# Products with adj by pairs of batches in seven half products, with one pool of PSUM banks

## The chip, the cores and the metric

The kernel runs on one core of a Trainium2 chip. The metric is the device time of one execution in microseconds (us), median of the runs in the fast state.

PE is TensorE, PEld its weight loads, DVE VectorE, ACT ScalarE, POOL GpSimd, SP the engine that issues the DMAs here (all but two loads of adj). PSUM is the memory that the kernel's matmuls write; its buffers there make eight banks of 512 fp32 columns. A record is one matmul entry of the trace; most fp32 matmuls leave two (1280 for the 640 product matmuls of the kernel before). L423 is line 423 of the kernel that the profile belongs to.

## The reference

Four graph layers on x (32 batches of 512 nodes and 128 features), each `x = x + layer(relu(layernorm(x)))`. The change concerns layer 1, a gated recurrence of five steps. Both of its matrices are `adj`, so a step needs one product with adj for each batch:

```python
def step(h, _):
    m_in = jnp.einsum('nm,bmd->bnd', in_matrix, h)      # in_matrix = out_matrix = adj
    m_out = jnp.einsum('nm,bmd->bnd', out_matrix, h)
    av = jnp.concatenate([m_in, m_out], axis=-1)
    u3 = h @ u3_w.T + u3_b
    z = jax.nn.sigmoid(av @ w3_w.T + w3_b + u3)
    r = jax.nn.sigmoid(av @ w4_w.T + w4_b + u3)
    hv = jnp.tanh(av @ w5_w.T + w5_b + (r * h @ u5_w.T + u5_b))
    h = (1.0 - z) * h + z * hv
    return (h, None)
h, _ = jax.lax.scan(step, input, None, length=time_step)   # five steps
```

Layer 0 is one normalized product with adj, layers 2 and 3 are graph attention. All is fp32.

## The kernel before

The kernel records every operation with an engine, an assumed cost, a due time and the values that it reads and writes. `Plan.run` then orders them once, when the program is built, as a list schedule. It hands out buffers as it goes, and the operations are emitted in that order. The tile framework adds the semaphore waits afterwards, from what the emitted instructions read and write.

```python
    plan = Plan({
        "bank": tiles(3, TOKENS, "bank", psum),
        "cand": tiles(1, TOKENS, "cand", psum),
        "wide": tiles(2, [P, C, 2 * P], "wide", psum),     # two banks each
        "lane": list(range(LANES)),                        # LANES = 4 batches in the recurrence at once
        ...
    def product(h, mT, due):
        p, m = Val("bank"), Val("m")
        for c in range(C):                                 # C = 4 chunks of 128 nodes
            op("PE", MM, due, lambda c=c: nc.tensor.matmul(flat(p.t), chunk(h, c), mT.t[:, c, :],
               start=(c == 0), stop=(c == C - 1)), ...)
        op("ACT", A, due, lambda: nc.scalar.copy(flat(m.t), flat(p.t)), r=[p], w=[m])
        return m
    ...
    def step(b, s, h, hT, due, lane):
        m = product(h, adjT, due)
        # PE: gate = w4*m + u3*hT   ACT: r = tanh(gate)   DVE: rh = (r + 1) * hT
        # PE: gate += w3*m (the same bank)   ACT: z = tanh(gate)
        # PE: cand = w5*m + u5*rh   ACT: hv = tanh(cand)   DVE: three operations make the new hT
        # DVE transpose, DMA out and in: h of the next step, floats of a chunk at stride four
```

The softmax here doesn't subtract the row's maximum and nothing guards it: scores larger than these inputs give would overflow.

## Time and profile before

The time was 1751.78 us (1751.01 to 1752.13, 4 runs).

| | before |
|---|---|
| PE busy | 99% of the span |
| DVE / ACT busy | 68% / 41% |
| start to start, fp32 record of 512 columns | 429 ns |
| start to start, record of 128 to 131 columns | 109 to 112 ns |
| weight load of h / of y | 308 / 190 ns (medians) |

The prediction below shows the lines. For PE, a duration in a group is a modelled latency, so its time is better read from the distance between starts. From each distance I subtracted what the columns take. That is an estimate, a line laid through the measured distances: 0.8333 x N + 2.3 ns for the N columns of a record. It gives 429 ns for 512 columns (measured 429), 111.5, 109.8 and 109.0 for 131, 129 and 128 (medians 112, shortest 111, 109 and 109), and in the changed kernel 215.6 for 256 (median 216). What remains is called excess below; I take it for the time in which PE had no columns to stream. It splits the span of 1749.9 us into 1687.8 of columns, 4.9 before the first matmul and 57.2 of excess: 15.5 in the first 100 us, 19.7 between 100 and 1600 us, 22.0 after.

### The profile page before, as it was taken

What the parts mean: (1) busy time and instruction counts of PE and PEld (TensorE: products, weight loads), DVE (VectorE), ACT (ScalarE), POOL (GpSimd) and SP (SyncE); (2) the same over time, 40 slices, a digit from 0 to 9 for tenths busy, and PEclk for the clock granted to TensorE, in tenths of its full rate; (3) what the DMA queues carried; (4) which work ended last, traced back from release to release, by engine and by line L of the source; (5) the groups of instructions that cost most, each with busy time, mean ns of one, the idle gap of its engine ahead of it and who ended that gap; (6) DMA issues with size and microseconds to landing.
All of it is one profiled execution on the core that took longest, in us unless ns stands there. A gap on an engine that the chain in (4) does not pass through costs nothing.

```text
span 1749.9 us, 20047 instructions
## 1 busy us (share of the span) xinstructions
PE 1724.1 (99%) x6256; PEld 1097.3 (63%) x6256; DVE 1182.3 (68%) x2853; ACT 711.4 (41%) x1389; POOL 184.5 (11%) x168
## 2 busy tenths in 40 slices
PE   7999999999999999999999999999999999999997
PEld 4555565756656666565666656666666666666576
DVE  8655566857767766585777756676767666666577
ACT  5433435334344343534344343344343443433342
POOL 5200001100101011110011110001100000000001
PEclk9999999999999999999999999999999999999999
DMA  6122223225233432323343233243233333333200
GB/s 187 37 66 66 67 72 100 76 69 141 69 102 87 107 103 67 98 75 78 100 109 103 73 81 89 61 114 99 71 86 88 91 95 83 83 91 87 59 6 25
DMA packets 199754, 146.96 MB, mean 84 GB/s; under 512 B 21600, under 2 KB 165088, under 8 KB 199648
## 3 DMA queue, kind: packets, MB, share of 16 engines
q1 hardware_dynamic: 199360, 145.16, 30.8%
q8 instruction: 49, 0.80, 0.2%
q10 hardware_dynamic: 288, 0.52, 0.1%
q14 instruction: 57, 0.47, 0.1%
HBM read 81.01 MB, written 64.60 MB: 83 GB/s over the span
## 4 chain that ended last, share of the span: by engine, by line
PE 96%; DVE 2%; ACT 1%; issue 0%; POOL 0%; DMA 0%; DVEq 0%; POOLq 0%; ACTq 0%
PE bank L423 38%; PE wide L559 13%; PE bank L467 8%; PE cand L474 8%; PE cand L475 8%; PE bank L460 8%; PE bank L461 8%; PE wide L524 3%; PE bank L439 2%; PE bank L403 1%; ACT y L387 0%; DVE e L552 0%; PE bank L544 0%; DMA e<-in_adj_dram 0%; PE bank L267 0%
## 5 line engine op out<-in xcount | busy, mean ns | idle before, releaser
L423 PE MATMUL bank<-adjT,h 128*128 128x512 f32 x1280 | 610.3, 603 | 3.2 <-ACT h L387 2.7
L423 PEld LDWEIGHTS bank<-adjT,h 128*128 128x128 f32 x1280 | 386.4, 310 | 166.8 <-issue 51.9
L479 DVE TENSOR_TENSOR hv<-hv,hT 128x512 f32<-128x512 f32 x160 | 111.2, 695 | 274.7 <-ACT hv L477 274.3
L377 POOL TENSOR_TENSOR rstd<-ve,mhalf 128x4 f32<-128x4 f32 x128 | 141.2, 1104 | 1341.8 <-DVE ve L375 1196.7
L559 PEld LDWEIGHTS wide<-h_gat,e 128*128 128x128 f32 x2048 | 241.2, 193 | 26.9 <-issue 20.6
L559 PE MATMUL wide<-h_gat,e 128*128 128x129 f32 x2048 | 242.3, 276 | 2.0 <-DVE v L565 2.0
L463 ACT ACTIVATE r<-bank,gate_bw 128x512 f32<-128x512 f32 x160 | 109.6, 685 | 257.0 <-PE bank L461 234.9
L425 ACT COPY m<-bank 128x512 f32<-128x512 f32 x192 | 112.1, 584 | 217.5 <-PE bank L423 217.1
L465 DVE SCALAR_TENSOR_TENSOR rh<-r,hT 128x512 f32<-128x512 f32 x160 | 110.3, 689 | 112.2 <-ACT r L463 111.5
L552 DVE SCALAR_TENSOR_TENSOR e<-row,h_gat,maskT 128x512 f32<-128x512 f32 x256 | 180.3, 744 | 2.9 <-DMA row<-line 2.5
L387 ACT ACTIVATE y<-x,off,rstd 128x128 f32<-128x128 f32 x384 | 163.2, 485 | 41.4 <-DVE off L384 21.8
L477 ACT ACTIVATE hv<-cand,gate_bw 128x512 f32<-128x512 f32 x160 | 109.7, 686 | 170.6 <-PE cand L475 170.6
L469 ACT ACTIVATE z<-bank,gate_bw 128x512 f32<-128x512 f32 x160 | 109.8, 686 | 149.5 <-PE bank L467 148.7
L467 PE MATMUL bank<-m,wT 128*128 128x512 f32 x320 | 163.9, 594 | 0.8 <-ACT r L463 0.8
L460 PE MATMUL bank<-m,wT 128*128 128x512 f32 x320 | 163.5, 593 | 0.7 <-ACT m L425 0.7
L474 PE MATMUL cand<-m,wT 128*128 128x512 f32 x320 | 163.4, 592 | 0.0
L461 PE MATMUL bank<-hT,wT 128*128 128x512 f32 x320 | 163.4, 592 | 0.0
L475 PE MATMUL cand<-rh,wT 128*128 128x512 f32 x320 | 163.4, 592 | 0.0
L411 DVE STREAM_TRANSPOSE sq<-hT 128x512 f32<-128x512 f32 x154 | 158.6, 1030 | 2.1
L423 PE MATMUL bank<-anT,y 128*128 128x512 f32 x256 | 121.8, 604 | 1.3 <-ACT y L387 1.3
L370 DVE BATCH_NORM_STATS2 st<-x 128x6 f32<-128x128 f32 x512 | 115.6, 278 | 2.2 <-DMA x<-in_x_dram 0.9
L482 DVE SCALAR_TENSOR_TENSOR hT<-hv,hT 128x512 f32<-128x512 f32 x160 | 112.0, 700 | 3.5
(90 smaller groups left out, 1307.8 us busy)
## 6 DMA issues: line engine op xcount, KB each, us to landing
far<-sq SPq DMA_DIRECT2D x840, 64.0 KB
h<-far SPq DMA_DIRECT2D x154, 256.0 KB
gT<-far SPq DMA_DIRECT2D x56, 256.0 KB
row<-line SPq DMA_DIRECT2D x56, 256.0 KB
x<-in_x_dram SPq DMA_DIRECT2D x32, 256.0 KB
out_dram<-x SPq DMA_DIRECT2D x32, 256.0 KB
far_mask<-mask SPq DMA_DIRECT2D x8, 128.0 KB
maskT<-far_mask SPq DMA_DIRECT2D x8, 128.0 KB
```

What stands on the lines that cost most here:

```text
L370: op("DVE", 0.21, due, lambda c=c: nc.vector.bn_stats(st.t[:, c, :], xb.t[:, c, :]), r=[xb[c]], w=[st[c]])
L377: op("POOL", 1.0, due, lambda: nc.gpsimd.tensor_tensor(rstd.t, ve.t, mhalf.t, ALU.pow), r=[ve, mhalf], w=[rstd])
L387: op("ACT", 0.32, due, lambda c=c: nc.scalar.activation(chunk(y, c), xb.t[:, c, :], AF.Relu, bias=off.t[:, c:c + 1], scale=rstd.t[:, c:c + ...
L411: op("DVE", 0.61 if form == "p q (c j) -> p q c j" else 1.0, soon, lambda: nc.vector.transpose(sq.t.rearrange(form, c=C), flat(src.t).rear ...
L423: op("PE", MM, due, lambda c=c: nc.tensor.matmul(flat(p.t), chunk(h, c), mT.t[:, c, :], start=(c == 0), stop=(c == C - 1)), r=[h[c] if len ...
L460: nc.tensor.matmul(flat(gate.t), gates.t[:, 0, :], flat(m.t), start=True, stop=False)
L461: nc.tensor.matmul(flat(gate.t), gates.t[:, 1, :], flat(hT.t), start=False, stop=True)
L467: op("PE", MM, due + 0.3, lambda: nc.tensor.matmul(flat(gate.t), gates.t[:, 2, :], flat(m.t), start=False, stop=True, skip_group_check=Tru ...
L474: nc.tensor.matmul(flat(cand.t), gates.t[:, 3, :], flat(m.t), start=True, stop=False)
L475: nc.tensor.matmul(flat(cand.t), u5T.t[:, 0, :], flat(rh.t), start=False, stop=True)
L552: op("DVE", 0.68, due + 3, lambda j=j: nc.vector.scalar_tensor_tensor(e.t[:, j, :], row.t, h.t[:, j, D + 1:D + 2], maskT[l].t[:, j, :], op ...
L559: nc.tensor.matmul(p.t[:, c, :D + 1], e.t[:, j, c * P:(c + 1) * P], h.t[:, j, :D + 1], start=(j == 0), stop=(j == C - 1))
```

## The change

Its intent is fewer columns on the full engine. Two batches of a step form a 2 x 2 block problem with adj, which one level of Strassen solves with seven half-size products in place of eight. The half products need four vector sums before and five after them. Six lanes (three pairs) replace four. Since a product now holds three banks, all eight banks become one pool: four tiles of two banks each, from which single banks and pairs are cut. h is laid out in pairs of floats. The shuttle of the diff is the transpose and the DMAs that turn the new hT into the next step's h.

```diff
-LANES = 4
+LANES = 6
@@ Plan.run
+        banks = [True] * (2 * len(self.buffers["psum"]))
+        def pick(v):
+            if v.kind == "wide":
+                return next(([i, i + 1] for i in range(0, len(banks), 2) if banks[i] and banks[i + 1]), None)
+            if v.kind == "bank":
+                some = [i for i, ok in enumerate(banks) if ok]
+                return [max(some, key=lambda i: (not banks[i ^ 1], i))] if some else None
+            return free[v.kind][-1:] or None
+        def take(v, slot):
+            ...
+                pair = self.buffers["psum"][slot[0] // 2]
+                v.t = pair if v.kind == "wide" else pair.rearrange("p (a c) (b k) -> p a (c b) k", a=2, b=2)[:, slot[0] % 2]
@@ buffers
-        "bank": tiles(3, TOKENS, "bank", psum),
-        "cand": tiles(1, TOKENS, "cand", psum),
-        "wide": tiles(2, [P, C, 2 * P], "wide", psum),
+        "psum": tiles(4, [P, C, 2 * P], "psum", psum),
@@ layout of h
-        return h.t.rearrange("p k (j c) -> p c (k j)", c=C)[:, c, :]
+        return h.t.rearrange("p a (f l) -> p a l f", l=2)[:, c // 2, c % 2, :]
@@ the bias add of layer 0 moves from POOL to DVE; the shuttle of h goes in two halves
@@ products of two batches
+        combine(S[2], x1[0], x2[0], sub)      # DVE, 128x256 each
+        combine(S[0], x2[0], x2[1], add)
+        combine(S[1], S[0], x1[0], sub)
+        combine(S[3], x1[1], S[1], sub)
+        times(r1, x1[0], 0, True, m1, m2, p1, u2, u4)      # PE, two matmuls of 256 columns each
+        op("ACT", ... copy(p1.t, low(r1)))
+        times(r2, S[1], 1, True)
+        op("DVE", ... tensor_add(u2.t, p1.t, low(r2)))
+        times(r3, S[0], 2, True)
+        op("DVE", ... tensor_add(u4.t, u2.t, low(r3)))
+        times(r1, x1[1], 3, False)
+        op("ACT", ... copy(low(m1), low(r1)))
+        times(r2, S[2], 4, True)
+        op("DVE", ... tensor_add(high(m2), u4.t, low(r2)))
+        times(r3, S[3], 5, False)
+        op("DVE", ... tensor_add(high(m1), u2.t, low(r3)))
+        times(r2, x2[1], 6, False)
+        op("DVE", ... tensor_add(low(m2), u2.t, low(r2)))
@@ (cut: seven factors of adj at the start, buffer counts, pairs in the main loop)
```

More of the change, by code (lines that the diff above doesn't have):

```diff
@@ L81, in run, with drop @@
     def run(self):
-        free = {k: list(reversed(v)) for k, v in self.buffers.items()}
+        free = {k: list(reversed(range(len(v)))) for k, v in self.buffers.items() if k != "psum"}
+        banks = [True] * (2 * len(self.buffers["psum"]))
[7 more added lines that the diff above has]
+        def take(v, slot):
+            v.slot = slot
+            if v.kind in ("wide", "bank"):
+                for i in slot:
+                    banks[i] = False
+                pair = self.buffers["psum"][slot[0] // 2]
+                v.t = pair if v.kind == "wide" else pair.rearrange("p (a c) (b k) -> p a (c b) k", a=2, b=2)[:, slot[0] % 2]
+            else:
+                free[v.kind].pop()
+                v.t = self.buffers[v.kind][slot[0]]
+        def drop(v):
+            if v.kind in ("wide", "bank"):
+                for i in v.slot:
+                    banks[i] = True
+            else:
+                free[v.kind].append(v.slot[0])
         ready = {e: [] for e in self.DELAY}
@@ L107, in start @@
                 opens = [v for v in o.vals if v.kind and v.t is None]
-                if all(free[v.kind] for v in opens):
-                    for v in opens:
-                        v.t = free[v.kind].pop()
+                got = []
+                for v in opens:
+                    if not (slot := pick(v)):
+                        break
+                    take(v, slot)
+                    got.append(v)
+                if len(got) < len(opens):
+                    for v in reversed(got):
+                        drop(v)
+                        v.t = None
+                else:
                     busy[e] = True
@@ L140, in run @@
                     if not v.uses and v.kind:
-                        free[v.kind].append(v.t)
+                        drop(v)
             for e in ready:
@@ L169, in gnn_stack @@
     plan = Plan({
-        "bank": tiles(3, TOKENS, "bank", psum),
-        "cand": tiles(1, TOKENS, "cand", psum),
-        "wide": tiles(2, [P, C, 2 * P], "wide", psum),
+        "psum": tiles(4, [P, C, 2 * P], "psum", psum),
         "lane": list(range(LANES)),
-        "x": tiles(16, TOKENS, "x"),
-        "h": tiles(LANES + 2, [P, Q, W * C], "h"),
+        "x": tiles(13, TOKENS, "x"),
+        "h": tiles(LANES + 1, [P, 2, 2 * D], "h"),
         "sq": tiles(2, [P, Q, W * C], "sq"),
         "far": tiles(4, [Q, W, Q, W * C], "far", dram),
-        "hT": tiles(2 * LANES, TOKENS, "hT"),
+        "hT": tiles(LANES + 3, TOKENS, "hT"),
         "y": tiles(3, TOKENS, "y"),
-        "m": tiles(LANES + 2, TOKENS, "m"),
+        "m": tiles(LANES + 1, TOKENS, "m"),
+        "S": tiles(2, [P, 4, 2 * D], "S"),
+        "half": tiles(6, [P, 2 * P], "half"),
         "r": tiles(2, TOKENS, "r"),
-        "rh": tiles(LANES, TOKENS, "rh"),
-        "z": tiles(LANES, TOKENS, "z"),
+        "rh": tiles(4, TOKENS, "rh"),
+        "z": tiles(4, TOKENS, "z"),
         "hv": tiles(2, TOKENS, "hv"),
@@ L198, in gnn_stack @@
         "rden": tiles(3, SMALL, "rden"),
-    }, 168, 0.1)
+    }, 172, 0.1)
     op = plan.op
@@ L257, in gnn_stack @@
                 a_pair[l].t[:, i:i + 1], column(a[f"L{l}_gnn_a_{k}"])), w=[a_pair[l][i]], delay=2.4)
-    adjT = fixed([P, C, N], "adjT", C)
+    adjT = Val("e", C)
     deg, dinv = fixed(SMALL, "deg", C), fixed(SMALL, "dinv")
@@ L296, in gnn_stack, with quarter, factor @@
     op("DVE", 4 * 0.7 + 4 * 0.25, -797, scale_rows, r=[adjT, dinv, drow, ident, dinv2], w=[anT])
+    half_adj = fixed([P, 7, 2, 2 * P], "half_adj", 7)
+    def quarter(a, n):
+        return adjT.t[:, 2 * a:2 * a + 2, n * 2 * P:(n + 1) * 2 * P]
+    def factor(k, out_of, *also):
+        op("DVE", 0.62, -795, lambda: out_of(half_adj.t[:, k]), r=[adjT, *[half_adj[i] for i in also]], w=[half_adj[k]])
+    for k, u, n in ((0, 0, 0), (3, 1, 0), (5, 1, 1)):
+        factor(k, lambda o, u=u, n=n: nc.vector.tensor_copy(o, quarter(u, n)))
+    factor(2, lambda o: nc.vector.tensor_sub(o, quarter(0, 1), quarter(0, 0)))
+    factor(1, lambda o: nc.vector.tensor_sub(o, quarter(1, 1), half_adj.t[:, 2]), 2)
+    factor(4, lambda o: nc.vector.tensor_sub(o, quarter(1, 1), quarter(0, 1)))
+    factor(6, lambda o: nc.vector.tensor_sub(o, quarter(1, 0), half_adj.t[:, 1]), 1)
     maskT = {l: fixed([P, Q, N], f"maskT{l}", C, dtype=BF16) for l in (2, 3)}
@@ L388, in norm_relu @@
                 chunk(y, c), xb.t[:, c, :], AF.Relu, bias=off.t[:, c:c + 1], scale=rstd.t[:, c:c + 1]),
-               r=[xb[c], off, rstd], w=[y[c]])
+               r=[xb[c], off, rstd], w=[y[c * len(y.writers) // C]])
     def chunk(h, c):
@@ L405, in to_features, with shuttle @@
         return p
-    def shuttle(src, squares, dst, form, due, soon):
+    def shuttle(src, squares, dst, halves, due, soon):
         sq, far = Val("sq"), Val("far", Q)
-        op("DVE", 0.61 if form == "p q (c j) -> p q c j" else 1.0, soon, lambda: nc.vector.transpose(
-            sq.t.rearrange(form, c=C), flat(src.t).rearrange(squares, c=C, q=Q)), r=[src], w=[sq])
+        if halves:
+            for a in range(2):
+                op("DVE", 0.34, soon, lambda a=a: nc.vector.transpose(
+                    sq.t.rearrange("p q (a j l) -> p a q l j", a=2, l=2)[:, a],
+                    flat(src.t).rearrange("p (a l q i) -> p a q l i", a=2, l=2, q=Q)[:, a]), r=[src], w=[sq])
+        else:
+            op("DVE", 0.61, soon, lambda: nc.vector.transpose(
+                sq.t.rearrange("p q (c j) -> p q c j", c=C), flat(src.t).rearrange(squares, c=C, q=Q)), r=[src], w=[sq])
         for k in range(Q):
@@ L415, in shuttle @@
                 far.t[:, :, k, :].rearrange("q i f -> i q f"), sq.t[k * W:(k + 1) * W]), r=[sq], w=[far[k]], delay=4)
-        op("SP", 0.4, due, lambda: nc.sync.dma_start(dst.t, far.t.rearrange("q i k f -> (q i) k f")),
-           r=[far], w=[dst], delay=5)
+        if halves:
+            for a in range(2):
+                op("SP", 0.4, due, lambda a=a: nc.sync.dma_start(
+                    dst.t[:, a, :].rearrange("p (k f) -> p k f", k=Q),
+                    far.t.rearrange("q i k (a f) -> a (q i) k f", a=2)[a]), r=[far], w=[dst[a]], delay=5)
+        else:
+            op("SP", 0.4, due, lambda: nc.sync.dma_start(
+                dst.t if dst.kind != "h" else dst.t.rearrange("p a (k f) -> p (a k) f", k=2), far.t.rearrange("q i k f -> (q i) k f")),
+               r=[far], w=[dst], delay=5)
     def product(h, mT, due):
@@ L431, in gcn @@
         norm_relu(b, y, due)
-        op("POOL", 1.3, due, lambda: nc.gpsimd.tensor_tensor(xb.t, xb.t, b0.t[:, None, :].to_broadcast([P, C, D]), ALU.add),
+        op("DVE", V, due + 1, lambda: nc.vector.tensor_add(xb.t, xb.t, b0.t[:, None, :].to_broadcast([P, C, D])),
            r=[b0], w=[xb])
@@ L441, in gcn @@
         op("DVE", V, due + 2, lambda: nc.vector.tensor_add(flat(xb.t), flat(xb.t), flat(p.t)), r=[p], w=[xb])
-    def ggnn(b, due):
-        xb, lane, h = xs[b], Val("lane"), Val("h", C)
-        op("SP", 0.0, due - 3, lambda: None, r=[xb], w=[lane], delay=0)
-        op("SP", 0.0, due - 3, lambda: None, r=[lane], w=[h], delay=0)
-        norm_relu(b, h, due - 3)
-        hT = Val("hT")
-        p = to_features(h, due - 2, hT)
-        op("ACT", A, due - 2, lambda p=p, hT=hT: nc.scalar.copy(flat(hT.t), flat(p.t)), r=[p], w=[hT])
-        for s in range(STEPS):
-            h, hT = step(b, s, h, hT, due + LANES * s, lane)
@@ L455, in step, with ggnn @@
-    def step(b, s, h, hT, due, lane):
-        m = product(h, adjT, due)
+    def ggnn(pair, due):
+        hs, hTs, lanes = [], [], []
+        for b in pair:
+            lane, h, hT = Val("lane"), Val("h", 2), Val("hT")
+            op("SP", 0.0, due - 3, lambda: None, r=[xs[b]], w=[lane], delay=0)
+            op("SP", 0.0, due - 3, lambda: None, r=[lane], w=[h], delay=0)
+            norm_relu(b, h, due - 3)
+            p = to_features(h, due - 2, hT)
+            op("ACT", A, due - 2, lambda p=p, hT=hT: nc.scalar.copy(flat(hT.t), flat(p.t)), r=[p], w=[hT])
+            hs.append(h)
+            hTs.append(hT)
+            lanes.append(lane)
+        for s in range(STEPS):
+            now = due + LANES * s
+            ms = products(*hs, now)
+            for i, b in enumerate(pair):
+                hs[i], hTs[i] = step(b, s, ms[i], hTs[i], now + i, lanes[i])
@@ new lines, in products, with part, combine, times @@
+    def products(h1, h2, due):
+        x1, x2, S = (h1[0], h1[1]), (h2[0], h2[1]), Val("S", 4)
+        HV, HM = 0.34, 2 * 0.43
+        def part(item):
+            v, a = item
+            return v.t[:, a, :]
+        def combine(o, u, v, f):
+            op("DVE", HV, due - 5, lambda: f(part(o), part(u), part(v)), r=[u, v], w=[o])
+        add, sub = nc.vector.tensor_add, nc.vector.tensor_sub
+        combine(S[2], x1[0], x2[0], sub)
+        combine(S[0], x2[0], x2[1], add)
+        combine(S[1], S[0], x1[0], sub)
+        combine(S[3], x1[1], S[1], sub)
+        m1, m2, p1, u2, u4 = Val("m", 2), Val("m", 2), Val("half"), Val("half"), Val("half")
+        r1, r2, r3 = Val("bank"), Val("bank"), Val("bank")
+        def times(r, item, k, fresh, *also):
+            def two():
+                u = part(item).rearrange("p (f l) -> p l f", l=2)
+                for l in range(2):
+                    nc.tensor.matmul(flat(r.t)[:, :2 * P], u[:, l, :], half_adj.t[:, k, l, :], start=fresh and l == 0, stop=l == 1,
+                                     skip_group_check=not fresh)
+            op("PE", HM, due, two, r=[item, half_adj], w=[r, *also])
+        def low(v):
+            return flat(v.t)[:, :2 * P]
+        def high(v):
+            return flat(v.t)[:, 2 * P:]
+        times(r1, x1[0], 0, True, m1, m2, p1, u2, u4)
+        op("ACT", 0.35, due, lambda: nc.scalar.copy(p1.t, low(r1)), r=[r1], w=[p1])
+        times(r2, S[1], 1, True)
+        op("DVE", HV, due - 5, lambda: nc.vector.tensor_add(u2.t, p1.t, low(r2)), r=[p1, r2], w=[u2])
+        times(r3, S[0], 2, True)
+        op("DVE", HV, due - 5, lambda: nc.vector.tensor_add(u4.t, u2.t, low(r3)), r=[u2, r3], w=[u4])
+        times(r1, x1[1], 3, False)
+        op("ACT", 0.35, due, lambda: nc.scalar.copy(low(m1), low(r1)), r=[r1], w=[m1[0]])
+        times(r2, S[2], 4, True)
+        op("DVE", HV, due - 5, lambda: nc.vector.tensor_add(high(m2), u4.t, low(r2)), r=[u4, r2], w=[m2[1]])
+        times(r3, S[3], 5, False)
+        op("DVE", HV, due - 5, lambda: nc.vector.tensor_add(high(m1), u2.t, low(r3)), r=[u2, r3], w=[m1[1]])
+        times(r2, x2[1], 6, False)
+        op("DVE", HV, due - 5, lambda: nc.vector.tensor_add(low(m2), u2.t, low(r2)), r=[u2, r2], w=[m2[0]])
+        return m1, m2
@@ L457, in step @@
+    def step(b, s, m, hT, due, lane):
         gate, r, rh, z = Val("bank"), Val("r"), Val("rh"), Val("z")
@@ L470, in step @@
            r=[gate, gate_b["w3"]], w=[z])
-        cand, hv, new = Val("cand"), Val("hv"), Val("hT")
+        cand, hv, new = Val("bank"), Val("hv"), Val("hT")
         def candidate():
@@ L485, in step @@
         last = s == STEPS - 1
-        if STEPS * b + LANES * s >= STEPS * B - EASE:
-            h = None if last else Val("h")
+        h = None if last else Val("h", 2)
+        if due >= STEPS * B - EASE:
             p = to_features(new, due + 2, *([] if last else [h]))
@@ L492, in step @@
             else:
-                op("ACT", A, due + 1, lambda: nc.scalar.copy(h.t.rearrange("p k (j c) -> p c (k j)", c=C), p.t), r=[p], w=[h])
+                for a in range(2):
+                    op("ACT", 0.35, due + 1, lambda a=a: nc.scalar.copy(
+                        h.t[:, a, :].rearrange("p (f l) -> p l f", l=2), p.t[:, 2 * a:2 * a + 2, :]), r=[p], w=[h[a]])
             return h, new
-        h = Val("h")
-        form = "p q (c j) -> p q c j" if last else "p q (j c) -> p q c j"
-        shuttle(new, "p (c q i) -> p q c i", h, form, due, due - 5)
-        if last:
-            op("DVE", V, due + 2, lambda: nc.vector.tensor_add(
-                xs[b].t.rearrange("p c (k j) -> p k c j", k=Q), xs[b].t.rearrange("p c (k j) -> p k c j", k=Q),
-                h.t.rearrange("p k (c j) -> p k c j", c=C)), r=[h, lane], w=[xs[b]])
-        return h, new
+        if not last:
+            shuttle(new, None, h, True, due, due - 5)
+            return h, new
+        h = Val("h", 2)
+        shuttle(new, "p (c q i) -> p q c i", h, False, due, due - 5)
+        op("DVE", V, due + 2, lambda: nc.vector.tensor_add(
+            xs[b].t.rearrange("p c (k j) -> p k c j", k=Q), xs[b].t.rearrange("p c (k j) -> p k c j", k=Q),
+            h.t.rearrange("p a (k c j) -> p (a k) c j", k=2, c=C)), r=[h, lane], w=[xs[b]])
+        return None, new
     def gat(b, l, due):
@@ L519, in gat @@
         else:
-            shuttle(y, "p (c q j) -> p q c j", gT, "p q (c j) -> p q c j", due + 0.5, due)
+            shuttle(y, "p (c q j) -> p q c j", gT, False, due + 0.5, due)
         def heads():
@@ L579, in gat @@
             op("SP", 0.95, due + 4, lambda: nc.sync.dma_start(out[b].rearrange("(c p) d -> p c d", p=P), xb.t), r=[xb])
-    for b in range(B):
-        gcn(b, STEPS * b - 8)
-        ggnn(b, STEPS * b)
-        gat(b, 2, STEPS * b + LANES * (STEPS - 1) + 3)
-        gat(b, 3, STEPS * b + LANES * (STEPS - 1) + 8)
+    for b in range(0, B, 2):
+        gcn(b, STEPS * b - 10)
+        gcn(b + 1, STEPS * b - 8)
+        ggnn((b, b + 1), STEPS * b)
+        for i in range(2):
+            gat(b + i, 2, STEPS * (b + i) + LANES * (STEPS - 1) + 3)
+            gat(b + i, 3, STEPS * (b + i) + LANES * (STEPS - 1) + 8)
     with tc.manual_schedule():
```

## The prediction

Its sum came to 1624 + 25 + 28 + 20 = 1697 us. That h at stride two would load in about 195 ns, on which "no stride loss" in the sum and the case against rival 2 rested, was the estimate. The 0.335 us of a half-size add can be had from the kernel before: adds of 128 columns start their successors after 0.202 us (L325), of 512 after 0.603 (L499, median), and a line between them gives 0.336 at 256.

> **What bounds the kernel now.** I read the page's busy shares and slices first, then its chain, then the costliest groups, then PE's timeline in mid-span and the busy time by stretches.
>
> ```profile
> PE 1724.1 (99%) x6256; PEld 1097.3 (63%) x6256; DVE 1182.3 (68%) x2853; ACT 711.4 (41%) x1389; POOL 184.5 (11%) x168
> ...
> PEclk9999999999999999999999999999999999999999
> ...
> PE 96%; DVE 2%; ACT 1%; issue 0%; POOL 0%; DMA 0%; DVEq 0%; POOLq 0%; ACTq 0%
> ```
>
> PE is busy throughout at full clock, and the chain is 96% PE. A busy PE need not be a full one, so I checked the pace. PE's timeline from 900 us:
>
> ```profile
> 900.50 2.74 PE L423 MATMUL bank<-adjT,h 128*128 128x512 f32 x6
> 903.07 1.02 PE L460 MATMUL bank<-m,wT 128*128 128x512 f32 x2
> 903.93 1.02 PE L461 MATMUL bank<-hT,wT 128*128 128x512 f32 x2
> 904.79 1.06 PE L524 MATMUL wide<-w_aug,gT 128*128 128x131 f32 x8
> 905.68 1.14 PE L423 MATMUL bank<-adjT,h 128*128 128x512 f32 x2
> 906.66 0.27 PE L544 MATMUL bank<-ident,h_gat 128*4 128x128 f32 x1
> ```
>
> The first column is the start. Six records of 512 columns take 903.07-900.50 = 2.57 us, 429 ns each; eight of 131 columns take 0.89 us, 112 ns each. So time on PE is columns alone, and each fp32 matmul leaves two records (1280 of L423 are 32 batches x 5 steps x 4 chunks x 2). One exception is visible: the pair at 905.68 takes 0.98 us, not 0.86, after short matmuls. The costliest groups say why:
>
> ```profile
> L423 PE MATMUL bank<-adjT,h 128*128 128x512 f32 x1280 | 610.3, 603 | 3.2 <-ACT h L387 2.7
> L423 PEld LDWEIGHTS bank<-adjT,h 128*128 128x128 f32 x1280 | 386.4, 310 | 166.8 <-issue 51.9
> ...
> L467 PE MATMUL bank<-m,wT 128*128 128x512 f32 x320 | 163.9, 594 | 0.8 <-ACT r L463 0.8
> ```
>
> In all groups with shapes kept apart, the same load from a contiguous source is shorter:
>
> ```profile
> L423 PEld LDWEIGHTS bank<-anT,y 128*128 128x128 f32 x256 | 47.6, 195 | 51.2 <-issue 46.4 <-ACT y L387 2.4 <-DVE x L441 0.7
> ```
>
> The mean of 603 ns is a modelled latency; I use starts. The weight load of h, whose elements stand four floats apart, takes 310 ns against 195. It hides behind a 429 ns matmul but not behind a 112 ns one. Counting starts in the trace, in 104 places a product follows a short matmul and its first record takes 550 ns instead of 429: 104 x 0.121 = 12.6 us. The last column shows that PE hardly waits for anyone in the whole run (3.2 us for L423). The ends differ, by stretches:
>
> ```profile
> 0.00:50.00 50.00, 38.17 (x119) 23.06 (x120) 42.12 (x203) 23.32 (x51) 25.15 (x29) 1.00 0.60 163
> 100.00:400.00 300.00, 300.00 (x900) 179.19 (x898) 185.15 (x400) 124.10 (x226) 23.04 (x21) 1.00 0.28 75
> 400.00:800.00 400.00, 399.35 (x1504) 257.76 (x1503) 280.30 (x677) 162.27 (x322) 44.79 (x39) 1.00 0.34 92
> 1700.00:1750.00 50.00, 39.19 (x297) 36.19 (x295) 40.79 (x109) 11.63 (x29) 4.71 (x4) 0.93 0.08 22
> ```
>
> (After the length: busy PE, PEld, DVE, ACT, POOL.) In the middle PE is full and DVE 70% busy; only the first and last 50 us leave PE idle, where the DVE is busier than PE.
>
> PE's account: 1280 + 1600 gate + 256 first-layer records = 3136 of 512 columns x 0.429 = 1345 us; 2816 of 128 to 131 columns x 0.112 = 315; 272 transposes x 0.11 = 30; together 1690. Stride losses are 12.6. The remaining 47 of 1750 are about 20 at the head, 22 at the tail, 5 between.
>
> [...]L467 writes the bank that ACT reads at L463, and lost 0.8 us in 160 turns.
>
> **The change, part by part.**
>
> Products with adj. Two batches took 2 x 4 x 2 = 16 records of 512 columns, 6.86 us. Now there are 7 half products x 2 chunks x 2 = 28 records of 256 columns. By the slope of the measured pair (512 and 128 columns) each is 429 - 256 x 0.833 = 215.7 ns, 6.04 us a pair step. Over 80 pair steps: 549.1 becomes 483, so -66 us on PE, which is the path. A weight load at 112 ns pace stays hidden behind 215.7.
>
> Layout of h in pairs (stride two). If loads run at the contiguous pace, the 104 penalties go: -12.6 us on the path. The DVE transposes into the shuttle, now 0.94 us start to start (written at stride four), should take 2 x 0.35, as those of y take 0.63: 124 x 0.24 = -30 us of DVE, off the path.
>
> Vector work added: nine half-size adds per pair step (four before, five after the products). A 128x512 add starts its successor after 0.60 us[...]; 256 fewer elements make 0.335. 80 x 9 x 0.335 = +241 us. The bias add of layer 0 moves from POOL (41 us) to DVE: 32 x 0.6 = +19. Seven factors of adj at the start: +3. DVE: 1182 + 241 + 19 + 3 - 30 = 1415 us, some 83% of the new span. Off the path while it keeps up.
>
> ACT: 160 copies of 0.58 become 160 of about 0.36: -36, off the path.
>
> Six lanes and one pool of banks: three pairs in flight. One pair's next step comes 6/10 of a pair's share of the span later, about 6 x 10.5 = 63 us; I estimate from the durations (product 6, gates 10 to 12, shuttle 12 to 15, sums 2) some 35 us for the chain itself. So PE should nearly always have another pair to work on.
>
> Sum: PE 1690 - 66 = 1624, no stride loss. Head 20 + 5: factors on a DVE that is already 84% busy there, and a first product that needs two batches. Tail 22 + 6: two batches instead of one finish last, with four attention layers left and nothing to fill. Between, 5 + 15 for PE waiting on a busier DVE. 1624 + 25 + 28 + 20 = 1697 us, 3.1% less.
>
> **The rivals.**
>
> 1. Turns of the banks inside a product. Three banks serve seven half products; the last use of the second bank waits for a DVE read with only one half product (0.86 us) to cover it, while a DVE add can stand behind an attention op of 0.74 us. If a pair step lost 0.5 us, 40 us more than the sum, about 1730. For it: DVE at 83%[...]. Against: L467's turn of the same kind loses 5 ns each, and other pairs' gates can stand between.
>
> 2. Weight loads at stride two no better than at stride four. I estimate a strided load at 112 + 121 = 233 ns pace, from the penalty. It would set the pace over 215.7: 2240 x 17 ns = +39, and the 12.6 stay: about 1748.[...]
>
> 3. DVE becomes the bound, or its queueing stretches the chain of three pairs until PE runs dry. 1415 us is below 1624, so only bursts can do it; it would make 1730 to 1760. The head and tail, with DVE at 42 and 41 of 50 us, are where it surely bites.
>
> 4. The schedule hides everything as today, head and tail keep their 42: about 1672.
>
> **Range and chances.** Rival 4 sets the low side, a mild form of 1 or 3 the high side: 1665 to 1733. Faster by over 2% means under 1716.9, 20 us above my sum; rivals 1 to 3 in earnest take a fifth of the chances. A loss needs over 1787, hardly possible unless DVE fails badly.
>
> **What would show it.** Right: the product's records 216 ns apart, weight loads of h near 195 ns, no 121 ns penalties, DVE busy near 1415, PE still 97% or more in mid-span with waits at the product under 15 us. Wrong: weight loads near 310; PE idle at the half products released by DVE adds of the sums (rival 1) or of the four first combinations (rival 3); PE below 95% in the middle; or a tail over 35 us.

## The result

The changed kernel took 1905.02 us (1902.87 to 1908.57, 4 runs). The ratio is 1.0877, 95% interval 1.0859 to 1.0896, so 8.8% slower. A ratio here is the mean time of one kernel's fast runs over that of the other's of the same rounds, so not quite the ratio of the medians quoted.

The page of the changed kernel, busy time, PE in 40 slices, and the chain:

```profile
PE 1737.3 (91%) x7224; PEld 1128.3 (59%) x7224; DVE 1372.1 (72%) x3734; ACT 661.0 (35%) x1394; POOL 140.2 (7%) x136
...
PE   6999989998999999999999999999998999999887
...
PE 55%; DVE 11%; ACT 7%; issue 2%; SPq 0%; DMA 0%; POOL 0%; DVEq 0%; ACTq 0%; POOLq 0%
```

PE fell from 99% to 91% of a longer span, and its share of the chain from 96% to 55%. No other engine took its place: DVE is at 72%, ACT at 35%, and the slices look alike from end to end. Stretches say the same. Columns are the length, then busy PE, PEld, DVE, ACT and POOL, granted clock, DMA share and GB/s. The kernel before:

```profile
100.00:1600.00 1500.00, 1498.53 (x5326) 946.43 (x5325) 1008.78 (x2323) 613.38 (x1192) 139.02 (x121) 1.00 0.32 87
```

The changed kernel:

```profile
0.00:100.00 100.00, 78.78 (x260) 45.83 (x260) 69.75 (x291) 38.92 (x85) 20.92 (x26) 1.00 0.33 90
100.00:1600.00 1500.00, 1389.45 (x5642) 891.96 (x5642) 1079.09 (x2877) 525.32 (x1096) 100.38 (x93) 1.00 0.32 80
1600.00:1800.00 200.00, 181.74 (x784) 119.73 (x783) 143.58 (x360) 64.36 (x137) 9.24 (x9) 0.99 0.29 73
1800.00:1907.00 107.00, 87.33 (x542) 70.78 (x540) 79.70 (x209) 32.43 (x76) 9.63 (x9) 0.91 0.09 25
```

In the same 1500 us PE is idle for 111 us instead of 1.5, with DVE and ACT far from full; head and tail are no longer the only thin places. The costliest groups of the changed kernel (after the bar: busy us, mean ns, then idle us before them with what ended most of it):

```profile
L551 PE MATMUL psum<-half_adj,S 128*128 128x256 f32 x1280 | 323.5, 388 | 27.2 <-DVE half L563 7.6
L551 PEld LDWEIGHTS psum<-half_adj,S 128*128 128x128 f32 x1280 | 241.2, 197 | 107.0 <-ACT z L589 17.7
...
L580 PE MATMUL psum<-m,wT 128*128 128x512 f32 x320 | 169.1, 610 | 26.5 <-DVE m L573 9.3
...
L587 PE MATMUL psum<-m,wT 128*128 128x512 f32 x320 | 168.4, 609 | 23.7 <-ACT r L583 18.4
```

The loads of the half products take 197 ns, as hoped, and their matmuls are 216 ns apart at the median. But most kinds of matmul have idle time before them, L580 and L587 too, which the change left alone; L587 is the second gate, which had 0.8 us before.

The account of the span by excess, in us:

| | before | changed |
|---|---|---|
| columns | 1687.8 | 1622.6 |
| before the first matmul | 4.9 | 4.7 |
| excess, 0 to 100 us | 15.5 | 31.4 |
| excess, 100 to 1600 us | 19.7 | 184.4 |
| excess, after 1600 us | 22.0 | 63.7 |
| span | 1749.9 | 1906.8 |

The columns fell by 65 us as intended. Excess rose by 222, and that is the loss. Between 100 and 1800 us alone it is now 216; before, it was 42 from 100 us to the end.

**A wait that no data asks for.** The first-layer product L487 multiplies y and a normalized adj and reads nothing of the recurrence. Yet these lines of its view in the changed kernel say what PE sat idle for before it, in us and times:

```profile
  ACT r L583: 24.5, 20
  ACT y L438: 11.0, 5
  ACT hv L597: 9.5, 8
  DVE m L573: 9.3, 10
```

y is its operand. r, hv and m belong to other batches. The timeline of the changed kernel shows one of them (start, length):

```profile
715.65 1.02 PE L581 MATMUL psum<-hT,wT 128*128 128x512 f32 x2
...
717.18 1.12 PE L487 MATMUL psum<-anT,y 128*128 128x512 f32 x2 [0.51 <-DVE m L573]
718.40 0.69 ACT L583 ACTIVATE r<-psum,gate_bw 128x512 f32<-128x512 f32 x1 [5.10 <-PE psum L487]
...
719.14 1.13 PE L487 MATMUL psum<-anT,y 128*128 128x512 f32 x2 [0.84 <-ACT r L583]
```

L581 has completed a gate at 716.67. ACT, idle, could read it then, but starts at 718.40, when the first piece of L487 is over. The next piece of the same L487 sum then waits until ACT has read. Two operations on different banks wait for each other. (The 0.51 us before the first piece are another matter: by the program, DVE was still reading that very bank.)

The built program tells why. For each wait I looked up the instruction that raises the semaphore to the awaited value and compared the PSUM addresses of the two. At 719.14 L487 writes the first bank of a pair tile, and the read that it waits for is of the second bank of that tile. Counts of such waits of PE for ACT and DVE, and of ACT and DVE for PE:

```
waits for an access to the other bank of the same pair tile     PE    ACT   DVE
before                                                          11      0     0
changed                                                        363    251   173
```

PE has some 1580 waits in all in the changed kernel. ACT and DVE also wait for each other in this way there, 66 and 65 times, which the table leaves out. That the framework places waits by the allocated pair is what the program shows; what in the framework does it I did not look into.

### The profile page after: what moved, and what is told of

Same layout as the page of the kernel before. It is cut to its first block, busy times and chain, and to the rows that moved or that the text cites. A ratio compares the mean times of both kernels' runs of the same rounds, so it can differ in the third digit from the quotient of the medians.

```text
span 1906.8 us, 23034 instructions
## 1 busy us (share of the span) xinstructions
PE 1737.3 (91%) x7224; PEld 1128.3 (59%) x7224; DVE 1372.1 (72%) x3734; ACT 661.0 (35%) x1394; POOL 140.2 (7%) x136
## 4 chain that ended last, share of the span: by engine, by line
PE 55%; DVE 11%; ACT 7%; issue 2%; SPq 0%; DMA 0%; POOL 0%; DVEq 0%; ACTq 0%; POOLq 0%
PE psum L551 15%; PE psum L682 8%; PE psum L580 5%; PE psum L587 5%; PE psum L594 5%; PE psum L581 5%; PE psum L595 5%; PE psum L487 3%; PE psum L647 2%; ACT r L583 2%; ACT y L438 2%; DVE e L675 1%; ACT hv L597 1%; DVE hv L600 1%; PE psum L503 1%
## 5 line engine op out<-in xcount | busy, mean ns | idle before, releaser
L551 PE MATMUL psum<-half_adj,S 128*128 128x256 f32 x1280 | 323.5, 388 | 27.2 <-DVE half L563 7.6
L551 PEld LDWEIGHTS psum<-half_adj,S 128*128 128x128 f32 x1280 | 241.2, 197 | 107.0 <-ACT z L589 17.7
L551 PE MATMUL psum<-half_adj,h 128*128 128x256 f32 x960 | 253.8, 390 | 25.6 <-DVE m L569 6.7
L682 PEld LDWEIGHTS psum<-h_gat,e 128*128 128x128 f32 x2048 | 239.9, 193 | 16.7 <-issue 10.0
L682 PE MATMUL psum<-h_gat,e 128*128 128x129 f32 x2048 | 243.0, 277 | 1.5 <-DVE e L675 0.8
L551 PEld LDWEIGHTS psum<-half_adj,h 128*128 128x128 f32 x960 | 179.7, 197 | 82.8 <-issue 15.2
L580 PE MATMUL psum<-m,wT 128*128 128x512 f32 x320 | 169.1, 610 | 26.5 <-DVE m L573 9.3
L587 PE MATMUL psum<-m,wT 128*128 128x512 f32 x320 | 168.4, 609 | 23.7 <-ACT r L583 18.4
L594 PE MATMUL psum<-m,wT 128*128 128x512 f32 x320 | 167.8, 606 | 9.2 <-ACT hv L597 6.4
L595 PE MATMUL psum<-rh,wT 128*128 128x512 f32 x320 | 164.2, 595 | 0.0
L581 PE MATMUL psum<-hT,wT 128*128 128x512 f32 x320 | 163.5, 592 | 0.0
L487 PE MATMUL psum<-anT,y 128*128 128x512 f32 x256 | 131.6, 618 | 25.1 <-ACT r L583 8.1
```

Source lines behind the costliest of these rows:

```text
L551: nc.tensor.matmul(flat(r.t)[:, :2 * P], u[:, l, :], half_adj.t[:, k, l, :], start=fresh and l == 0, stop=l == 1, skip_group_check=not fresh)
L580: nc.tensor.matmul(flat(gate.t), gates.t[:, 0, :], flat(m.t), start=True, stop=False)
L581: nc.tensor.matmul(flat(gate.t), gates.t[:, 1, :], flat(hT.t), start=False, stop=True)
L587: op("PE", MM, due + 0.3, lambda: nc.tensor.matmul(flat(gate.t), gates.t[:, 2, :], flat(m.t), start=False, stop=True, skip_group_check=Tru ...
L594: nc.tensor.matmul(flat(cand.t), gates.t[:, 3, :], flat(m.t), start=True, stop=False)
L595: nc.tensor.matmul(flat(cand.t), u5T.t[:, 0, :], flat(rh.t), start=False, stop=True)
```

## The experiments

Three theories. **A**: the waits for the other bank of a pair make the stalls. **B** (the prediction's first rival): the turns of the banks inside a product, with a busier DVE. A turn is a wait of PE until ACT or DVE has read the very bank that PE is to write next. **C**: six lanes in pairs bring work too late. All eight results were correct. "Before" ran at 1751.66 and 1751.72 us in their two groups.

| run | median us | ratio to before | 95% interval |
|---|---|---|---|
| e1_eight | 1679.07 | 0.9583 | 0.9569 to 0.9597 |
| e2_fixed | 1680.80 | 0.9596 | 0.9582 to 0.9610 |
| e3_pool_only | 2029.95 | 1.1584 | 1.1567 to 1.1602 |
| e4_whole | 1740.82 | 0.9935 | 0.9919 to 0.9952 |
| e5_spread | 1703.13 | 0.9723 | 0.9709 to 0.9738 |
| e9_before_eight | 1752.12 | 1.0006 | 0.9989 to 1.0023 |
| e8_layout | 1748.51 | 0.9980 | 0.9965 to 0.9995 |
| e7_lanes4 | 1745.75 | 0.9970 | 0.9955 to 0.9985 |

### e1_eight: the changed kernel with eight single-bank tiles

```diff
-        "psum": tiles(4, [P, C, 2 * P], "psum", psum),
+        "psum": tiles(8, TOKENS, "psum", psum),
-                pair = self.buffers["psum"][slot[0] // 2]
-                v.t = pair if v.kind == "wide" else pair.rearrange(...)[:, slot[0] % 2]
+                own = [self.buffers["psum"][i] for i in slot]
+                v.t = own[0] if v.kind == "bank" else [t.rearrange("p (c b) k -> p c (b k)", b=2) for t in own]
@@ the four operations of attention that span two banks are written as two, as here
-        nc.vector.reciprocal(rden.t, p.t[:, :, D])
+        [nc.vector.reciprocal(rden.t[:, 2 * i:2 * i + 2], p.t[i][:, :, D]) for i in range(2)]
```

> The changed kernel with the same order of work and the same banks, but each PSUM bank is a tile of its own (eight tiles instead of four pairs; an operation that spans two banks is written as two). Theory A, false waits: in the program of the changed kernel 363 of some 1580 waits of PE are for a read of the other bank of the same pair tile, which PE does not touch; with eight tiles there is none. A expects the 216 us of PE stalls in mid-span to fall under 30 and the time to be 1680 to 1710. Theory B, real turns of the banks inside a product and a busier DVE: nothing of that is changed, so 1890 to 1910. Theory C, six lanes in pairs bring work too late: 1890 to 1910.

It took 1679.07 us, 4.2% less than before and 1 us under the range that A gave. I compared the two programs: PE's 3766 matmul instructions stand in the same order, with the same operands, on the same banks and offsets. Only waits differ (and ACT and DVE have 64 and 160 instructions more). PE's groups now:

```profile
L551 PE MATMUL psum<-half_adj,S 128*128 128x256 f32 x1280 | 310.5, 380 | 0.5 <-DVE half L565 0.4 <-DVE half L563 0.2
...
L580 PE MATMUL psum<-m,wT 128*128 128x512 f32 x320 | 163.8, 593 | 0.0
...
L587 PE MATMUL psum<-m,wT 128*128 128x512 f32 x320 | 163.1, 592 | 0.0
...
L487 PE MATMUL psum<-anT,y 128*128 128x512 f32 x256 | 124.8, 605 | 4.4 <-ACT y L438 4.4
```

The idle time of 27, 26 and 24 us before L551, L580 and L587 is gone, and L487 waits for its own operand alone. The stretch of the middle:

```profile
100.00:1600.00 1500.00, 1496.72 (x6466) 1031.35 (x6465) 1225.81 (x3395) 603.69 (x1298) 114.76 (x104) 1.00 0.35 89
```

DVE is busier here than in the changed kernel (82% of the middle against 72%), because more work fits into the same time, and PE hardly waits (98% of the span, 96% of the chain). So B falls: the same sums and turns on the same three banks cost half a microsecond at L551. C falls too.

### e2_fixed: the changed kernel without the pool

```diff
-        "psum": tiles(4, [P, C, 2 * P], "psum", psum),
+        "bank": tiles(4, TOKENS, "bank", psum),
+        "wide": tiles(2, [P, C, 2 * P], "wide", psum),
@@ Plan.run hands out buffers as the kernel before does
```

> The changed kernel without the pool: four single banks and two wide pairs, as the kernel before has them; half products and six lanes stay. A (false waits): 1685 to 1720, a little more than with eight tiles since a product's three banks now compete for four. B (turns of the banks, busier DVE): 1900 or more, since fewer banks make the turns tighter. C (six lanes): about 1900.

1680.80 us, 1.7 more than e1 and 4 under the range that A gave. The pool was hardly needed at all: the split of before serves the half products as well.

### e3_pool_only: the kernel before with the pool of pair tiles alone

```diff
-        "bank": tiles(3, TOKENS, "bank", psum),
-        "cand": tiles(1, TOKENS, "cand", psum),
-        "wide": tiles(2, [P, C, 2 * P], "wide", psum),
+        "psum": tiles(4, [P, C, 2 * P], "psum", psum),
@@ and Plan.run of the changed kernel
```

> The kernel before with the pool of pair tiles alone: whole products, four lanes. Its program has 317 waits of PE and 356 of ACT for the other bank of a pair. A (false waits): clearly slower than before, 1850 to 1950, with PE stalls spread over the whole span. B and C, which blame the half products or the lanes: 1745 to 1760, as before.

2029.95 us, 15.8% more, beyond what I gave. Its costliest group, the product with adj, which sat idle for 3.2 us in the kernel before:

```profile
L457 PE MATMUL psum<-adjT,h 128*128 128x512 f32 x1280 | 678.4, 639 | 120.8 <-ACT r L497 54.9 <-ACT hv L511 27.5 <-ACT m L459 20.5
```

r and hv are no operands of this product. The half products are not needed for the loss. Why it is larger here than in the changed kernel (278 us over before, against 226 between the changed kernel and e1) I did not settle; the number of waits is not larger (317, 356 and 14 for PE, ACT and DVE).

### e4_whole: eight tiles, six lanes, whole products

```diff
-            ms = products(*hs, now)
+            ms = [product(h, adjT, now) for h in hs]
@@ on e1_eight, without the factors of adj
```

> Eight single tiles, six lanes and pairs as in the first of these runs, but whole products with adj (no half products, no vector sums). A: no false waits, so the lanes and the pool are harmless: PE has 66 us more matmul time than the first run, 1740 to 1765; the difference to the first run is what the half products are worth, 55 to 66 us less what the DVE gives back. B: 1740 to 1765 too, but then the first run is near 1900. C (six lanes): over 1800.

1740.82 us. Between this and e1 lie 61.8 us, the worth of the half products with the same lanes, layout and banks, though in an order that is made anew; in columns it is 1688.7 - 1622.6 = 66.1.

### e5_spread: pair tiles, but an empty pair first

```diff
-                return [max(some, key=lambda i: (not banks[i ^ 1], i))] if some else None
+                return [max(some, key=lambda i: (banks[i ^ 1], i))] if some else None
```

> The changed kernel with pair tiles, only the rule by which a bank is chosen turned round: a bank whose partner is free is taken first, where the change takes one whose partner is in use. The program then has 148 waits of PE for the other bank of a pair instead of 363, and 29 instead of 251 of ACT. A (false waits cost the time): a part of the 226 us between the changed kernel and its eight-tile form comes back, and the loss shrinks at least with the number of waits: 1690 to 1775. If instead only the presence of pair tiles mattered, by whatever way: near 1900.

1703.13 us: one word less gives back 202 of the 226 us. The rule of the change takes a bank whose partner is in use, to keep whole pairs free for attention; with pair tiles that puts strangers together as often as can be. Of the waits in the table, 148 of 363 are left for PE, 29 of 251 for ACT and 14 of 173 for DVE.

### e9_before_eight: the kernel before with a pool of eight single tiles

```diff
+        "psum": tiles(8, TOKENS, "psum", psum),
@@ on e3_pool_only, with the edits of e1_eight
```

> The kernel before with the pool as eight single tiles: PE's instructions stand in the same order on the same banks as in the run with the pool of pair tiles alone, which took 2030 us. A: a pool costs nothing by itself, 1747 to 1757. If the order or the choice of banks that a pool gives were at fault and not the waits: near 2030.

1752.12 us, within noise of before. PE's 3278 matmul instructions are in the order and on the banks of e3. So 278 us hang on the waits and not on the order or the banks.

### e8_layout: the kernel before with h in pairs of floats alone

```diff
-        "h": tiles(LANES + 2, [P, Q, W * C], "h"),
+        "h": tiles(LANES + 2, [P, 2, 2 * D], "h"),
-        return h.t.rearrange("p k (j c) -> p c (k j)", c=C)[:, c, :]
+        return h.t.rearrange("p a (f l) -> p a l f", l=2)[:, c // 2, c % 2, :]
@@ and the shuttle in two halves
```

> The kernel before with the stride-two layout of h alone (two halves per step, four lanes, whole products, PSUM as before). The prediction put 12.6 us on the weight loads of h at stride four after short matmuls and 30 us of DVE off the path. If that holds: weight loads of h near 195 ns, no 550 ns starts, 1736 to 1744. If loads at stride two are slow too, or the penalty was no loss: 1748 to 1755.

1748.51 us, 0.2% less, which counts as the same. It misses the 1736 to 1744 of the first case and falls into the range of the second. Yet the load itself did what was expected:

```profile
L436 PEld LDWEIGHTS bank<-adjT,h 128*128 128x128 f32 x1280 | 243.3, 196 | 260.7 <-issue 255.9 <-DMA far<-sq 1.2 <-DMA h<-far 0.7
```

It takes 196 ns instead of 310, and the late starts after short matmuls fell from 102 (12.2 us) to 1. The excess between 100 and 1600 us fell by 10.3 us, but after 1600 us it rose by 5.7 and in the first 100 by 1.1. The order is made anew for every kernel, and this one has a worse tail.

### e7_lanes4: e1 with four lanes

```diff
-LANES = 6
+LANES = 4
```

> The eight-tile form with four lanes instead of six, so two pairs in flight instead of three. If a pair step's chain is so long that two pairs leave PE without work now and then, as the change assumes: 1720 to 1780 with PE idle in mid-span at waits for sums and gates. If four lanes suffice: 1675 to 1690.

1745.75 us, 66.7 more than e1. With two pairs in flight PE runs out of work. The half products in this run, those of S and those of h:

```profile
L551 PE MATMUL psum<-half_adj,S 128*128 128x256 f32 x1280 | 317.5, 387 | 17.5 <-DVE S L538 8.9 <-DVE half L563 5.1 <-DVE half L565 2.9
L551 PE MATMUL psum<-half_adj,h 128*128 128x256 f32 x960 | 249.6, 383 | 11.9 <-ACT half L561 7.5 <-DMA h<-far 2.0 <-ACT h L438 1.2
```

Of these, S (L538) is an operand: 8.9 us. No half product reads a half. L561, L563 and L565 are the reads of the product's own banks, so 15.5 us are the turns of rival 1, which cost 0.5 us with six lanes. With too little other work in flight they do cost. The excess between 100 and 1600 us is 64.2 us against 14.2, after 1600 us 38.3 against 19.6. With four lanes the change gains 6 us (e7 against e9, which has the pool alone); with six, the half products gain 62 (e1 against e4).

## Why the prediction was wrong

**PE's account was right.** Predicted 1624 us of matmul time without stride loss, 216 ns a record and loads near 195 ns; the trace has 1622.6 (its records, each at the pace above), 216 and 197. The estimate for stride two held: 196 ns in e8, where stride four took 308 and the contiguous y 190 in the kernel before.

**The step that failed** is "Six lanes and one pool of banks": it went on to count pairs in flight and gave the pool no cost. I read the diff as a change of who may use which bank, and took the wait of L467 (0.8 us in 160 turns) as what a turn costs. In the program the unit of a wait is the allocated tile, and the pool made tiles of two banks that strangers share (363 such waits of PE). Its place in the sum is "Between, 5 + 15 for PE waiting on a busier DVE". Measured between 100 and 1800 us: 216.

**How the 222 us of added excess come about.** I matched PE's records one by one with the program's instructions. Of 267 us in gaps of over 30 ns in the changed kernel, 73 lie at starts where all waits are for the other bank, 23 where some are, 123 at starts with real waits only, and 48 at records that wait for nothing. Of the 123, by the addresses, 62 are at starts that wait only until the very bank has been read and 38 at starts that wait only for an operand. That these reads and operands were late because ACT and DVE stand in 424 such waits for PE themselves is an inference; what is shown is that with no such wait, in e1, the gaps are 38 us in all. The 48 are a cost of stopping: of 372 records that come 80 to 140 ns late without a wait, 361 follow a stalled start. At such a start the timeline has both weight loads of the matmul beginning with it, as at 719.14 above, where they take 0.30 us from the same moment (in the kernel before each is fetched under the matmul ahead: at 801.81 us the load for the record of L474 that starts at 802.24).

**Rival 1 fell** with e1: same turns, 0.5 us. In the changed kernel its sign had come, since the first releaser named at L551 is the sum L563 (7.6 us), and so had PE below 95% in the middle (1389 of 1500 us) and a tail over 35 us. A named releaser was not yet the cause. **Rival 2 fell**: loads at stride two took 197 ns, not 308. **Rival 3**, DVE as the bound, fell: DVE at 82% in e1 stops nobody (PE is busy 1496.72 of the 1500 us). Rival 4, "hides everything", gave 1672; e1 took 1679. What I would have had to name as a rival is a wait that the program adds without need.

**Vector work** was put at 1415 us busy; it is 1372 in the changed kernel and 1368 in e1. One add of 256 columns was put at 0.335 us from start to start, which is the median in the changed kernel. A size was off by 3%, without effect on the time. Whether a source was in PSUM made no difference to these adds: in the changed kernel the groups with one source there took 411 to 417 ns, those with none 413 to 415.

**Head and tail**, put at 25 and 28 us, are 21.8 (4.7 + 17.1) and 19.6 in e1, and the middle 14.2 instead of 20. That is why e1 lies 18 us below the predicted 1697. In the changed kernel itself they are 36 and 64, since the same waits act there.

**Slips of the working**: rival 1's "about 1730" should read 1737 (1697 + 40). DVE's 70% in the middle was that of 400 to 800 us alone; over 100 to 1600 us it was 67%. The slope of 0.833 belongs to the pair of 512 and 131 columns (317 ns over 381 columns, 0.832), not 128. None of them touches the failed step.

**The stride losses**, 12.6 us, were of the right size in the middle (10.3 in e8). That the whole of them would show in the time is not shown: e8 gave 3.2 us, its tail took back most.

**The six lanes** were right: two pairs leave PE without work (e7), three do not (e1).

## What to carry to other kernels

When a change regroups buffers, ask by what unit the waits are placed: merging two independent banks into one allocation can join two chains that have nothing in common (here 363 waits of PE, and 226 us between the changed kernel and e1), and here no other engine's load showed it (DVE 72%, ACT 35%). The sign in a profile is a wait on an engine whose result is no operand of the waiting instruction and which did not use its bank, on groups that the change did not touch, with no engine full. Here the cure cost a few extra instructions, and made a change of +8.8% one of -4.2%.
